# Warm-up products, an earlier half of the exponentials, and moved transposes in an attention and expert kernel on Trainium2

## The chip, the cores and the metric

The kernel runs on one core of a Trainium2 chip. The metric is device time in microseconds (us), the median of several executions; three of the kernel before took 761.15, 761.35 and 762.45 us. A profile is one further look at one execution. The engines have short names in it: PE is TensorE's matmul, PEld its weight load, DVE VectorE, ACT ScalarE, POOL GpSimd, SP the engine that issues most transfers.

## The reference

Sixteen batches of 128 tokens with 256 features pass two stages, all in fp32.

Stage one is attention of a resampler. `x` is normalised (plain layer norm) and becomes the latents; these and a context of the same size are layer-normed again with weights and biases, and the latents are modulated by a condition vector. Queries come from the latents, keys and values from context and latents together (256 rows a batch), in 16 heads of width 64:

```python
logits = jnp.einsum('bhqd,bhkd->bhqk', q * attn_scale, k * attn_scale)
w = jax.nn.softmax(logits.astype(jnp.float32), axis=-1)
out = jnp.einsum('bhqk,bhkd->bhqd', w, v)
```

The heads are projected back to 256 features and added to `x`.

Stage two is a mixture of experts on the layer norm of that: a router picks one of 8 experts for each token, its sigmoid score scales the token, and the expert computes `(silu(t @ w1) * (t @ w3)) @ w2` with 704 hidden columns. A shared expert of the same shape runs over every token. Both are added to the tokens.

## The kernel before, in words

Every engine's order is the order in which the Python code calls its operations: nothing is scheduled afterwards. Waits between engines follow from the tiles.

**Front.** Two batches make a group; there are eight. The first group's tokens and the weights of keys (`wk`), values, queries and output are loaded by SP and ACT. `first_inputs(i)` (from line 368) takes the i-th batch of the first group: statistics and a Newton square root on DVE, normalised rows `fz` (L126), four transposes on PE (L396), and scale and shift on DVE (L402) and ACT (L404) into `kvT`. In between stand the four key units of batch 0. `inputs(1)` prepares the rows of the second group; their transposes are in `second_inputs`, which calls `transpose` (L345 to L357: eight transposes on PE, six scalings on DVE) and starts the next loads.

**Units.** `k_unit` (L432) makes two of eight pairs of heads' keys: four fp32 products of 256 columns, shown as eight PE records, into one PSUM tile, which ACT copies to `kT` (L440). `v_unit` (L451, copy L458) and `q_unit` (L417, copy L424) do it for values and queries. All these tiles come from one PSUM pool, `ps_m`, with three buffers: the fourth tile waits until the first was emptied. A matmul of the first tokens' transposes, of the output projection and of the shared expert takes its tile from this pool too.

**Steps.** `step(u, units, ...)` handles half of the heads of one batch, so 32 steps. PE computes scores `S` in two tiles (L484). DVE takes maxima (`nmx`, L496), ACT the exponentials (`pe`, L503) with their sums, DVE the reciprocals (`rs`, L513), POOL the scaling (L516). Two halves (`n` = 0 and 1) pass this one after the other. `turn` transposes the probabilities in 32x32 blocks on DVE (L525) and stores them; `fetch` loads them back as `pT`; one step later `weigh` multiplies them by the values (`O`, L549). Between these, `step` calls one unit at a time so that PE has work: one after the first half's exponentials, one after the second half's, one after the second `normalise`, further ones before `turn`, the last after it.

**Last group.** In steps 28 to 31 there are no keys and queries of a next group left, and units of the shared expert fill in: `hidden` (products `p`, `pr` at L148, Silu into `sl` on ACT at L163 and L168, product `mid` on DVE at L164 and L169). Exp and Silu are in different tables of ACT, and a change is an `ACT_TABLE_LOAD`. A one-element exponential (`spare`, L792) opens each of these steps and brings Exp's table back early. `finish` is the output projection (`pw`, L565, added at L569); `norms` puts the layer norm of earlier tokens on DVE as side work.

**After it** come the rest of the shared expert (`ys`, L178, is its down projection), the routing on DVE, and 20 tiles of 128 sorted tokens through the experts (`u`, L1156, and `yr`, L1208), whose weights are loaded when attention's buffers are free.

Of the kernel before, what the change touches and what calls it, by code (L numbers as in the profile page):

```python
# [9 lines left out]
F32 = mybir.dt.float32  # L10
# [7 lines left out]
P = 128  # L18
EPS = 1e-5
RSQRT_SEED = float(0x5F3759DF)  # L20
G = 128


@with_exitstack
def resampler_attn__then__top1_moe_kernel(
# [17 lines left out]
    nc = tc.nc  # L43
# [8 lines left out]
    FC = F // P  # L52
# [4 lines left out]

    NSUB = NT // G + E - 1
    NTILE = -(-NSUB * G // P)
    GP = P // G  # L60
    TB = 2 * P
# [3 lines left out]
    NF = FC + 1  # L65
    assert G == P and NF % 2 == 0 and FR == 2 * BL and F <= 512 * 2

# [3 lines left out]
    mwork = ctx.enter_context(tc.tile_pool(name="mwork", bufs=2, side="right"))  # L71
    ps_s = ctx.enter_context(tc.tile_pool(name="ps_s", bufs=2, space=PSUM))
    ps_m = ctx.enter_context(tc.tile_pool(name="ps_m", bufs=3, space=PSUM))
# [10 lines left out]
            }  # L84
        )
    )

    ident = const.tile([P, P], F32, name="ident")
    make_identity(nc, ident)
# [17 lines left out]
    def newton(pool, v, n, tag):  # L107
# [5 lines left out]
        yi = pool.tile([P, n], I32, tag=tag + "i", name=tag + "i")  # L113
        nc.vector.tensor_scalar(yi, seed, -1.0, RSQRT_SEED, ALU.mult, ALU.add)
        y = yi.bitcast(F32)
# [129 lines left out]
    with ExitStack() as at:  # L245
# [226 lines left out]
        def logits(u):  # L472

            b, half = u // 2, u % 2
            pes[u] = work.tile([P, HS, 2 * S], F32, tag="pe", name=f"pe_{u}")
            sums[u] = small.tile([P, HS], F32, tag="sums", name=f"sums_{u}")
            ps = []
            for n in range(2):
                pl = ps_s.tile([P, 2, 2, 2 * S], F32, tag="S", name=f"S_{u}_{n}")
                for j in range(2):  # L480
                    k = 4 * half + 2 * n + j
                    for r in range(2):
                        rows = slice(r * HD, (r + 1) * HD)
                        nc.tensor.matmul(  # L484
                            pl[:, r, j, :],
                            lhsT=qTs[b // 2][rows, k, b % 2, :],
                            rhs=kTs[b][rows, k, :],
                            start=True,
                            stop=True,
                        )  # L490
                ps.append(pl)
            return ps

        def maxima(u, n, pl):
            nmx = small.tile([P, 2, 2], F32, tag="nmx", name=f"nmx_{u}_{n}")
            nc.vector.tensor_reduce(nmx, pl, AX.X, ALU.max, negate=True)  # L496
            return nmx

        def exponents(u, n, pl, nmx):
            for j in range(2):  # L500
                for r in range(2):
                    h = 4 * n + 2 * j + r
                    nc.scalar.activation(  # L503
                        pes[u][:, h, :],
                        pl[:, r, j, :],
                        AF.Exp,
                        bias=nmx[:, r, j : j + 1],
                        accum_out=sums[u][:, h : h + 1],
                    )

        def normalise(u, n):
            rs = small.tile([P, 4], F32, tag="rs", name=f"rs_{u}_{n}")
            nc.vector.reciprocal(rs, sums[u][:, ts(n, 4)])  # L513
            for i in range(4):
                w = pes[u][:, 4 * n + i, :]
                nc.gpsimd.tensor_scalar(w, w, rs[:, i : i + 1], None, ALU.mult)  # L516

        def turn(u, n):

            px = work.tile([P, NB, 2, HS // 2, BL], F32, tag="px", name=f"px_{u}_{n}")
            for t in range(2):
                nc.vector.transpose(  # L525
                    px[:, :, t].rearrange("p j h q -> p h j q"),
                    pes[u][:, ts(n, 4), ts(t, S)].rearrange("p h (j k) -> p h j k", k=BL),
                )
            nc.sync.dma_start(
                out=p_blocks[u % 2][n].rearrange("i k j x -> (i k) (j x)"),  # L530
                in_=px.rearrange("p j t h q -> p (j t h q)"),
            )

        def fetch(u):
            pTs[u] = work.tile([P, 2, NB, 2, HS // 2, BL], F32, tag="pT", name=f"pT_{u}")
            for n in range(2):
                nc.sync.dma_start(
                    out=pTs[u][:, n].rearrange("p i t h q -> p i (t h q)"),
                    in_=p_blocks[u % 2][n].rearrange("i k j x -> (k j) i x"),
                )  # L540
# [17 lines left out]
        def keep_heads(u):  # L558
            outT[u] = work.tile([P, NP // 2, S], F32, tag="oT", name=f"oT_{u}", bufs=3)
            nc.vector.tensor_copy(outT[u], heads_out.pop(u))  # L560

        def finish(b):
            pw = ps_m.tile([P, D], F32, tag="mm", name=f"pw_{b}")
            for k in range(NP):
                nc.tensor.matmul(  # L565
                    pw, lhsT=outT[2 * b + k // 4][:, k % 4, :], rhs=wo[:, k, :], start=(k == 0), stop=(k == NP - 1)
                )
            xr = xres[b // 2][:, b % 2, :]
            nc.vector.tensor_tensor(xr, pw, xr, ALU.add)  # L569
# [201 lines left out]
            a, b, c, fetch, d = [x + y for x, y in zip(t, h)]  # L771
            return a, b + ([iterate] if nt + nh else []), c, fetch, d

        def step(u, units, side, loads=(), early=4, behind=()):

            units, side = list(units), list(side)

            def aside(n):  # L780
                for f in side[:n]:
                    f()
                del side[:n]

            def unit():
                if units:
                    units.pop(0)()

            ps = logits(u)
            if u // 2 >= B - 2:  # L790

                nc.scalar.activation(spare[0:1, 1:2], spare[0:1, 0:1], AF.Exp)  # L792
            if u > 1:
                keep_heads(u - 2)
            nm = maxima(u, 0, ps[0])
            exponents(u, 0, ps[0], nm)
            nm = maxima(u, 1, ps[1])
            unit()
            for f in loads:
                f()  # L800
            normalise(u, 0)
            exponents(u, 1, ps[1], nm)
            unit()
            normalise(u, 1)
            aside(early)
            unit()
            aside(len(side))
            while len(units) > 1:
                unit()
            turn(u, 0)  # L810
            turn(u, 1)
            fetch(u)
            for f in behind:
                f()
            unit()
            if u > 0:
                weigh(u - 1)
# [21 lines left out]
        for g in range(NG):  # L839
            b0, b1 = 2 * g, 2 * g + 1  # L840
            q = [lambda j=j: q_unit(g + 1, j) for j in range(4)]
            k1 = [lambda j=j: k_unit(b1, j) for j in range(4)]
            v1 = [lambda j=j: v_unit(b1, j) for j in range(4)]
            k2 = [lambda j=j: k_unit(b1 + 1, j) for j in range(4)]
            v2 = [lambda j=j: v_unit(b1 + 1, j) for j in range(4)]
            wo_before = [lambda: finish(b0 - 1)] if g else []
            wo_first = [lambda: finish(b0)]
            na, nb, nn, back, nd = norms(g + 2 if g + 2 < NG else None, g - 1 if g else None)
            if g == 0:
                step(0, k1 + [second_inputs] + q[:2], [])  # L850
                load_shared()
                v1 = [lambda j=j: v_unit(0, j) for j in range(1, 4)] + v1
                na, nb = [], na + nb
            elif g + 1 < NG:
                step(2 * b0, k1 + q[:2] + choose, na)
            if g + 1 < NG:
                step(2 * b0 + 1, v1[:2] + wo_before + v1[2:], nb, early=0 if g else 4)
                step(2 * b1, k2 + q[2:], nn)
                ahead = [lambda: load_tokens(g + 3)] if g + 3 < NG else []
                step(2 * b1 + 1, v2[:2] + wo_first + v2[2:], [], back + ahead, behind=nd)  # L860
            else:

                sh = [shared_unit]
                step(2 * b0, k1 + sh * 2 + choose, [])
                step(2 * b0 + 1, sh * 2 + wo_before + sh * 3, nb, early=0)
                step(2 * b1, v1 + sh * 2, nn)
                step(2 * b1 + 1, sh * 2 + wo_first + sh, [], back, behind=nd)
            choose = [moe_inputs(g - 1)[2]] if g else []
        keep_heads(2 * B - 2)
        for j in range(NP // 2):  # L870
# [59 lines left out]
    def route():  # L930
# [66 lines left out]
        tiles_i = mscratch.tile([P, E], I32, name="tiles_i")  # L997
        nc.vector.tensor_scalar(tiles_i, total, float(G - 1), None, ALU.add)
        nc.vector.tensor_scalar(tiles_i, tiles_i, G.bit_length() - 1, None, ALU.arith_shift_right)
        tiles = mscratch.tile([P, E], F32, name="tiles")  # L1000
# [344 lines left out]
```

## Time and profile before

| what | us |
|---|---|
| median of three executions | 761.35 |
| the profiled execution | 762.45 |
| its span, first to last instruction | 760.6 |
| PE busy | 743.1 |
| POOL, DVE, ACT busy | 315.1, 414.1, 264.3 |
| first transposes on PE start | 7.87 |
| first key products start | 9.39 |
| step 29's scores start | 452.38 |

A timeline row gives the start, the time that the row covers, the engine, the line in the code, the operation, what it writes and reads, shapes and the number of instructions merged; in brackets stands how long the engine was idle before it and what ended the wait. A row of the waits gives who waited for whom: the sum in us, the number of times and the longest. A PE record lasts longer than the distance to the next one, since matmuls overlap; what a stream costs is read from the distance of starts.

### The profile page before, as it was taken

Reading aid. Unit: us, or ns where it says so; the run is one execution under the profiler, and the core shown is the slowest. Engines: PE = TensorE matmul, PEld = TensorE weight load, DVE = VectorE, ACT = ScalarE, POOL = GpSimd, SP = SyncE. Lnnn points to the kernel's source line nnn. Section 1 sums busy time; section 2 is a strip of 40 time slices with the busy share of each in tenths; the row PEclk is TensorE's granted clock in tenths of the full one; section 3 lists DMA queues with packets and bytes.
Section 4 is the critical chain, followed back from the end, with each engine's and each line's share of the span. In section 5 each row is a group of like instructions: output and inputs, shape, how many; then the busy total and the mean of one; then the engine's idle time right before and its main releaser. Section 6 shows DMA issues by size and latency. Waiting matters only on the chain.

```text
span 760.6 us, 11735 instructions
## 1 busy us (share of the span) xinstructions
PE 743.1 (98%) x4044; PEld 569.8 (75%) x4044; DVE 414.1 (54%) x1011; ACT 264.3 (35%) x783; POOL 315.1 (41%) x366
## 2 busy tenths in 40 slices
PE   5999999999999999999999999999999999999997
PEld 4758678677677677677677686788888777777776
DVE  4466558548647647656646456434732555555431
ACT  2544544444354353354354355711311111011111
POOL 1273464464355355445545544531012334443331
PEclk9999999999999999999999999999999999999999
DMA  8075734844943943863853644632997576776751
GB/s 291 1 238 194 221 124 160 264 146 153 262 168 134 279 170 125 240 218 125 226 200 131 185 151 140 201 139 88 383 381 261 131 200 182 212 190 184 184 155 55
DMA packets 182066, 142.48 MB, mean 187 GB/s; under 512 B 95152, under 2 KB 165811, under 8 KB 182004
## 3 DMA queue, kind: packets, MB, share of 16 engines
q1 hardware_dynamic: 175460, 125.07, 52.7%
q0 software_dynamic: 4528, 13.18, 5.5%
q10 hardware_dynamic: 2016, 3.43, 1.3%
q8 instruction: 35, 0.57, 0.3%
q14 instruction: 27, 0.22, 0.1%
HBM read 84.50 MB, written 57.67 MB: 187 GB/s over the span
## 4 chain that ended last, share of the span: by engine, by line
PE 73%; DMA 14%; DVE 4%; issue 4%; ACT 3%; POOL 1%; POOLq 0%; DVEq 0%; ACTq 0%; SPq 0%
PE pk L432 15%; PE pv L451 14%; PE S L484 7%; PE pq L417 7%; DMA out_dram<-sg,table 7%; PE O L549 7%; PE pw L565 6%; PE p L148 6%; DMA sg<-s_rows,table 5%; PE ys L178 4%; PE u L1156 3%; ACT pe L503 1%; DVE px L525 1%; PE yr L1208 1%; ACT L163 1%
## 5 line engine op out<-in xcount | busy, mean ns | idle before, releaser
L516 POOL TENSOR_SCALAR pe<-pe,rs 128x256 f32<-128x256 f32 x256 | 232.9, 931 | 255.3 <-DVE rs L513 255.3
L503 ACT ACTIVATE pe<-S,nmx 128x256 f32<-128x256 f32 x256 | 118.9, 489 | 133.0 <-DVE nmx L496 133.0
L432 PE MATMUL pk<-kvT,wk 128*128 128x256 f32 x512 | 117.4, 388 | 0.4 <-DVE kvT L402 0.4
L451 PE MATMUL pv<-wv,kvT 128*128 128x512 f32 x256 | 116.5, 599 | 0.8 <-ACT v L458 0.6
L432 PEld LDWEIGHTS pk<-kvT,wk 128*128 128x128 f32 x512 | 97.8, 194 | 18.9 <-DVE px L525 2.0
L1156 PE MATMUL u<-w13s,xT 128*128 x320 | 97.8, 459 | 0.0
L525 DVE STREAM_TRANSPOSE px<-pe 128x512 f32<-128x512 f32 x128 | 81.2, 682 | 29.6 <-POOL pe L516 29.6
L451 PEld LDWEIGHTS pv<-wv,kvT 128*128 128x128 f32 x256 | 47.2, 190 | 54.4 <-issue 51.1
L1156 PEld LDWEIGHTS u<-w13s,xT 128*128 128x128 f32 x320 | 60.8, 190 | 30.7
L496 DVE TENSOR_REDUCE nmx<-S 128x4 f32<-128x1024 f32 x64 | 75.1, 1214 | 9.4 <-PE S L484 9.4
L148 PE MATMUL p<-hT,ws 128*128 128x256 f32 x320 | 73.6, 382 | 0.8 <-DVE mid L164 0.5
L148 PEld LDWEIGHTS p<-hT,ws 128*128 128x128 f32 x320 | 59.9, 190 | 10.4 <-ACT v L458 1.2
L549 PEld LDWEIGHTS O<-pT,v 128*64 128x64 f32 x1024 | 55.2, 137 | 15.5 <-issue 12.9
L1166 ACT ACTIVATE rsl<-u 128x352 f32<-128x352 f32 x40 | 18.6, 464 | 130.6 <-PE u L1156 121.5
L484 PE MATMUL S<-kT,qT 64*128 64x256 f32 x512 | 63.9, 389 | 0.0
L549 PE MATMUL O<-pT,v 128*64 128x128 f32 x1024 | 63.2, 276 | 0.5 <-DMA pT<-p_blocks 0.5
L513 DVE RECIPROCAL rs<-sums 128x4 f32<-128x4 f32 x64 | 11.3, 177 | 91.8 <-ACT pe L503 91.8
L458 ACT COPY v<-pv 128x512 f32<-128x512 f32 x64 | 38.1, 601 | 62.9 <-PE pv L451 62.9
L417 PE MATMUL pq<-kvT,wq 128*128 128x256 f32 x256 | 58.0, 380 | 1.3 <-DVE kvT L357 1.3
L565 PE MATMUL pw<-wo,oT 128*128 128x256 f32 x256 | 57.9, 379 | 0.0
L565 PEld LDWEIGHTS pw<-wo,oT 128*128 128x128 f32 x256 | 48.6, 190 | 12.2 <-issue 3.1
L503 ACT ACTIVATION_READ_ACCUMULATOR pe<-S,nmx 128x1 f32 x256 | 56.3, 220 | 0.0
(201 smaller groups left out, 779.5 us busy)
## 6 DMA issues: line engine op xcount, KB each, us to landing
p_blocks<-px SPq DMA_DIRECT2D x64, 512.0 KB, 3.2
pT<-p_blocks SPq DMA_DIRECT2D x64, 512.0 KB, 4.2
w13s<-in_w_dram SPq DMA_DIRECT2D x16, 704.0 KB, 11.1
m_blocks<-body SPq DMA_DIRECT2D x20, 384.0 KB, 2.5
mT<-m_blocks SPq DMA_DIRECT2D x20, 384.0 KB, 3.8
wds<-in_w_dram SPq DMA_DIRECT2D x8, 640.0 KB, 12.4
t_blocks<-tx SPq DMA_DIRECT2D x12, 256.0 KB, 2.8
kvT<-t_blocks SPq DMA_DIRECT2D x12, 256.0 KB, 5.8
```

The source lines that it names most:

```text
L148: nc.tensor.matmul(ps, lhsT=shared["w13"][:, c, ds(col, P)], rhs=hT[:, c, ts(t, TB)], start=(c == 0), stop=(c == DC - 1),)
L417: nc.tensor.matmul(pq[:, jj], lhsT=wq[:, c, ts(2 * j + jj, P)], rhs=kvTs[g][:, c, :, 1, :], start=(c == 0), stop=(c == DC - 1),)
L432: nc.tensor.matmul(pk[:, jj, :], lhsT=wk[:, c, ts(2 * j + jj, P)], rhs=kvTs[b // 2][:, c, b % 2].rearrange("p t s -> p (t s)"), start=(c = ...
L451: nc.tensor.matmul(pv, lhsT=kvTs[b // 2][:, c, b % 2, t, :], rhs=wv[:, c, ts(n, 512)], start=(c == 0), stop=(c == DC - 1),)
L484: nc.tensor.matmul(pl[:, r, j, :], lhsT=qTs[b // 2][rows, k, b % 2, :], rhs=kTs[b][rows, k, :], start=True, stop=True,)
L496: nc.vector.tensor_reduce(nmx, pl, AX.X, ALU.max, negate=True)
L503: nc.scalar.activation(pes[u][:, h, :], pl[:, r, j, :], AF.Exp, bias=nmx[:, r, j : j + 1], accum_out=sums[u][:, h : h + 1],)
L516: nc.gpsimd.tensor_scalar(w, w, rs[:, i : i + 1], None, ALU.mult)
L525: nc.vector.transpose(px[:, :, t].rearrange("p j h q -> p h j q"), pes[u][:, ts(n, 4), ts(t, S)].rearrange("p h (j k) -> p h j k", k=BL),)
L549: nc.tensor.matmul(o[r * HD : (r + 1) * HD, j, :], lhsT=vs[b][:, t, ts(2 * (4 * half + j) + r, HD)], rhs=pTs[u][:, j // 2, :, t, 2 * (j % ...
L565: nc.tensor.matmul(pw, lhsT=outT[2 * b + k // 4][:, k % 4, :], rhs=wo[:, k, :], start=(k == 0), stop=(k == NP - 1))
L1156: nc.tensor.matmul(pl[:, m, 0:FH], lhsT=xT[:, c, :], rhs=w13s[:, ds(e, 1), c, ds(m * F + n * FH, FH)].rearrange("p e f -> p (e f)"), start ...
```

## The change

Three edits. First, ahead of everything else a tile is set to zero on DVE and PE multiplies it nine times by itself into a PSUM tile that nobody reads; the tile takes one of the two buffers that later hold `mid`. Second, `step` has a new argument `exp_first`: with it the first half's `normalise` and the second half's exponentials are called before the first unit instead of after it. Steps 29 and 31 use it, and in step 30 one of two shared units goes between the second and third value unit. Third, in step 0 `second_inputs` is called after the second of four key units rather than after the fourth.

```diff
+WARM = 9
...
+    idle = mwork.tile([P, FC + 1, TB], F32, tag="mid", name="idle")
+    nc.vector.memset(idle[:, 0, :], 0.0)
+    idle_ps = ps_m.tile([P, TB], F32, tag="mm", name="idle_ps")
+    for _ in range(WARM):
+        nc.tensor.matmul(idle_ps, lhsT=idle[:, 0, 0:P], rhs=idle[:, 0, :], start=True, stop=True)
...
-        def step(u, units, side, loads=(), early=4, behind=()):
+        def step(u, units, side, loads=(), early=4, behind=(), exp_first=False):
...
             nm = maxima(u, 1, ps[1])
+            if exp_first:
+                normalise(u, 0)
+                exponents(u, 1, ps[1], nm)
             unit()
             for f in loads:
                 f()
-            normalise(u, 0)
-            exponents(u, 1, ps[1], nm)
+            if not exp_first:
+                normalise(u, 0)
+                exponents(u, 1, ps[1], nm)
             unit()
...
-                step(0, k1 + [second_inputs] + q[:2], [])
+                step(0, k1[:2] + [second_inputs] + k1[2:] + q[:2], [])
...
-                step(2 * b0 + 1, sh * 2 + wo_before + sh * 3, nb, early=0)
-                step(2 * b1, v1 + sh * 2, nn)
-                step(2 * b1 + 1, sh * 2 + wo_first + sh, [], back, behind=nd)
+                step(2 * b0 + 1, sh * 2 + wo_before + sh * 3, nb, early=0, exp_first=True)
+                step(2 * b1, v1[:2] + sh + v1[2:] + sh, nn)
+                step(2 * b1 + 1, sh * 2 + wo_first + sh, [], back, behind=nd, exp_first=True)
```

## The prediction

> **What bounds the kernel now.** First the page's busy times, then the waits of PE, then the timeline at the three places that the diff touches.
>
> ```profile
> PE 743.1 (98%) x4044; PEld 569.8 (75%) x4044; DVE 414.1 (54%) x1011; ACT 264.3 (35%) x783; POOL 315.1 (41%) x366
> ```
>
> ```profile
> PE fkvt L396 <- DVE fz L126: 7.9, 1, 7.9
> PE pq L417 <- DVE kvT L357: 1.3, 2, 0.9
> PE pr L148 <- DVE mid L164: 0.8, 1, 0.8
> PE pv L451 <- ACT v L458: 0.6, 1, 0.6
> PE O L549 <- DMA pT<-p_blocks: 0.5, 1, 0.5
> ...
> PE ys L178 <- DVE mid L164: 0.4, 1, 0.4
> ```
>
> PE is occupied for 98% of the span, and its waits after the first add up to some 5 us. So PE sets the end, and time is won only where PE stands still or runs slowly. Two of the three edits aim at these waits, the third at slow running, which the waits do not show. First tokens:
>
> ```profile
> 7.87 1.13 PE L396 MATMUL fkvt<-ident,fz 128*128 128x128 f32 x4 [7.87 <-DVE fz L126]
> 9.39 9.78 PE L432 MATMUL pk<-kvT,wk 128*128 128x256 f32 x32 [0.40 <-DVE kvT L402]
> ...
> 30.59 7.17 PE L432 MATMUL pk<-kvT,wk 128*128 128x256 f32 x32
> ```
>
> The same 32 records take 9.78 us at the start and 7.17 us later: 2.6 us lost. Cut into stretches, the first of these runs shows 6 records in 10 to 12 and in 12 to 14 us, and 10 and 11 in the next two stretches; single starts lie 0.427 us apart until 14.7, then 0.216. Next the transposes of group two, between step 0's key and query units:
>
> ```profile
> 35.19 0.64 ACT L440 COPY kT<-pk 128x512 f32<-128x512 f32 x1
> ...
> 38.37 0.27 PE L346 MATMUL kvt<-ident,z 128*128 128x128 f32 x1
> ...
> 39.57 0.67 PE L417 MATMUL pq<-kvT,wq 128*128 128x256 f32 x2 [0.93 <-DVE kvT L357]
> 40.56 3.29 PE L417 MATMUL pq<-kvT,wq 128*128 128x256 f32 x14 [0.33 <-DVE kvT L357]
> ```
>
> The queries wait for VectorE to scale the tile just transposed. Last, step 29:
>
> ```profile
> 456.87 1.28 ACT L163 ACT_TABLE_LOAD   x1
> 458.16 0.38 ACT L163 ACTIVATE sl<-p 128x256 f32<-128x256 f32 x1
> 458.56 1.28 ACT L503 ACT_TABLE_LOAD   x1
> 458.58 0.42 DVE L164 TENSOR_TENSOR mid<-p,sl 128x256 f32<-128x256 f32 x1 [2.63 <-ACT sl L163]
> 458.92 0.17 DVE L513 RECIPROCAL rs<-sums 128x4 f32<-128x4 f32 x1
> ...
> 464.00 1.13 PE L148 MATMUL pr<-hT,ws 128*128 128x256 f32 x4 [0.80 <-DVE mid L164]
> 464.20 3.63 POOL L516 TENSOR_SCALAR pe<-pe,rs 128x256 f32<-128x256 f32 x4 [1.30 <-DVE rs L513]
> ```
>
> ScalarE goes to Silu's table and back between the two halves of the exponentials, and the first reciprocal (458.92) stands, in VectorE's order, behind a product that waits for that Silu, though its sums were there at 456.9.
>
> **What the Trainium skill says.** "TensorE: Matmul & The Clock Gate", section Part 1: TensorE runs at half rate until a window of about 3.4 us was busy; the windows run freely. The trace agrees on half rate (0.427 against 0.216). Part 4 there: transposes do not count as busy. That fits: the rate doubled 5.3 us after the first product of keys, 6.8 after the first transpose. "ScalarE: Activation LUTs", What ACT_TABLE_LOAD costs: 1.283 us plus 1.38 of drain. The trace shows 1.28, and no drain beside it (458.16 follows 456.87 by 1.29).
>
> **Part 1, nine products.** A memset on VectorE, which has nothing before 3.61; then nine fp32 products of 256 columns. 16 such products in four key units are 32 records, so nine are 18. The memset of 128x256 on VectorE has no row; POOL's 64x256 takes 0.34, VectorE's scaling of 128x256 0.41; so PE starts near 1.3. At 0.427 all 18 take 7.7 and end at 9.0, 1.1 past 7.87. But if one full window suffices, it closes between 1.3+3.4=4.7 and 1.3+6.8=8.1. By then 8 to 16 records are done, the rest take 0.216: the end lies between 6.9 and 8.5. Then the four transposes lie 0.109 apart, as the second batch's at 19.01 do, against 0.24. The second half of the normalised tokens is there at 8.04, so the first pair ends 0.19 earlier than before and keys start at 9.2 (in the late case at 9.65). 32 x 0.216 = 6.9, so they end at 16.1 to 16.6, against 19.0: **2.4 to 2.8 us, I take 2.6**. Below: if zeros do not count, the products only delay, by 1.1. Above: nothing more, as keys wait for VectorE's 7.63 + 0.41 and its scaling. What comes next is there: the loads of value and query weights landed at 11.2 and 14.2, wk at 8.3. Tokens of group two landed at 18.3; VectorE, which would be at them at 18.2, loses 0.1 at most, off the path.
>
> **Part 2, group two's transposes after the second key unit.** No instruction is added; VectorE's, ScalarE's and SP's orders stay. Lost now: 38.37+0.11 to 39.57, and 40.0 to 40.56, together 1.6. That goes, since the third and fourth key units (3.45) cover the six scalings (2 us). But the pool of PSUM tiles has three buffers: the two transposes' tiles take two, and the third key unit must wait for ScalarE's copy of the second, which stands behind the second half's exponentials and ends at 35.19 + 0.64 = 35.83. PE is there at 30.59 + 16 x 0.216 + 8 x 0.11 + 0.1 = 35.0. So 0.85 comes back as a new wait, with all of PE's order behind it (the two key units, both queries, step 1's scores); ScalarE and VectorE, who wait for these, have nothing due sooner: **0.75 won**. Low end 0.4, should the copy's hand-over cost more; high end 1.6. The tokens' load for the third group on SP stands where it did, ahead of the first blocks' stores.
>
> **Part 3, exponentials first (steps 29 and 31) and one shared unit between value units (step 30).** Two table loads fewer in each step, 4 x 1.28 on ScalarE, which is not the bound; only PE's waits count. I follow step 29, the start held at 452.38. Exponentials end at 456.83 and 458.7 instead of 461.8; load until 460.0; both Silus by 460.8; the two products on VectorE end at 460.9 and 461.3. First reciprocal 456.9 (was 458.92). The second now stands behind the two products, 461.3 (was 463.86); so POOL's second half starts at 461.7 instead of 464.20. PE has its fifth unit at 461.31 and the sixth at 463.04 without the wait: **0.96 won** (starts of 462.83 and 464.00, less 0.22). VectorE's norm work, 4.5 us in series from 463.95, starts at 461.6 since the output projection is done; so the maxima of step 30 come at 470.5 instead of 472.85, 1.4 earlier against PE. There the value copies now come in time, and PE's 0.75 (476.62) and 0.49 (478.93) go. The shared unit put between costs: its tile is freed only after table load and Silu, 478.7, and PE wants it at 478.3: 0.4 back. Sum **0.8**. Step 31: the exponentials start 2.8 earlier; the Silus are over by 490.8, so the down projection does not wait (0.68 at 496.75). The last probabilities: POOL ends at 495.4 instead of 500.6, VectorE's transposes at 496.75; from 501.9 to landing before 508.93 are 7.0, so they land at 503.8, and PE wants them at 504.9: the 0.79 at 508.93 goes. Together 0.96 + 0.8 + 0.68 + 0.79 = **3.2, I take 3.0**. Ends: 1.0, if only the first wait goes; 3.6 without the 0.4. After it PE stands for 0.5 us in all from 600 on, and the expert loads are issued after the same work, so they shift along.
>
> **Sum.** 2.6 + 0.75 + 3.0 = 6.3. The profiled execution took 762.45, its span 760.6; it would take 756.1. The median shown is 761.35, 1.1 lower: **755.0**.
>
> **Rivals.** *A, the clock.* Zeros do not open the gate, or it falls shut between the last product (6.9) and the keys (9.2): at most 2.4 us with nothing but transposes, less than a window. Then the front gains nothing or costs up to 1.1: 757.6 to 758.7. *B, buffers.* Step 29's Silu starts 1.9 later, so PSUM tiles come free later; by my count at 460.9 against a want at 461.3, only 0.4 to spare. If VectorE's order eats that, part 3 gives 1.2: 756.8. *C, slower.* The gate stays shut long after the gap. Part 1 of the skill's TensorE page reports a gate stuck for over 50 us; no run here shows it. At half rate PE loses half of the time. Against the 3.75 of parts 2 and 3, the slow stretch must last 7.5 us longer than now, beyond 22.2 instead of 14.7; from there the kernel is slower. With 30 us more it would lose 15 less 3.75: 772.6.
>
> **How the numbers follow.** Likeliest 0.68 (own range 753.6 to 756.6), A 0.13, B 0.14, no effect of any part 0.02, C 0.03. The range 753.4 to 758.4 takes in A mostly and B. Faster by over 0.2% (1.5 us, what a measurement can tell): 0.68 + 0.13 + 0.12 = 0.93; same 0.04; slower 0.03.
>
> **What would show it.** Right: the first 32 key records in about 7.0 us, from 9.2; a new wait of PE in the third key unit for ScalarE of 0.8 and none at the first queries; in steps 29 and 31 one table load after eight exponentials; no wait of PE for mid or for the last probabilities. Wrong: 0.427 spacing after 9.2 (A), PE waiting in steps 29 to 31 for mid or v (B), a long stretch at half rate (C).

## The result and the profile after

| | before | after |
|---|---|---|
| median of six executions, us | 761.49 | 755.98 |
| lowest to highest | 760.87 to 763.08 | 755.33 to 756.15 |
| span of the profiled execution | 760.6 | 753.6 |

The ratio is 0.9923, with a 95% interval of 0.991 to 0.9936: the kernel is 0.77% faster, 5.5 us by the medians and 4.9 to 6.9 by the interval. The forecast was 755.0, range 753.4 to 758.4. The spans of the two profiled executions differ by 7.0, which is 1.5 more than the medians: the profiled execution of before (762.45) lies 0.96 above the median of its six, that of after (755.33) 0.65 below. The experiments show where a part of this comes from.

Where did the time of the two profiles go? The starts of the stages on PE say it, in us from the span's start.

| from, to | before | after | won |
|---|---|---|---|
| start to step 0's scores | 28.66 | 25.80 | 2.87 |
| step 0's scores to step 1's | 15.12 | 14.32 | 0.80 |
| step 1's scores to step 29's | 408.59 | 408.59 | 0.00 |
| step 29's scores to step 30's | 16.31 | 15.25 | 1.06 |
| step 30's scores to step 31's | 15.79 | 14.89 | 0.90 |
| step 31's scores to the first expert tile | 105.31 | 104.07 | 1.24 |
| first expert tile to the end | 170.85 | 170.70 | 0.15 |

The page's busy times of the kernel after, then its waits of PE (who waited for whom: sum in us, times, longest):

```profile
PE 744.9 (99%) x4062; PEld 572.3 (76%) x4062; DVE 414.9 (55%) x1012; ACT 258.9 (34%) x779; POOL 315.2 (42%) x366
```

```profile
PE fkvt L404 <- DVE fz L134: 0.8, 1, 0.8
PE pk L440 <- ACT kT L448: 0.7, 1, 0.7
PE p L156 <- DVE mid L172: 0.7, 2, 0.5
```

The 18 records more are the nine products. Of the waits seen before, those of the queries (`pq`), of `pr`, `pv`, `O` and `ys` are gone. The wait of `pk` for ScalarE's `kT` is new, and so is one for `mid` in step 30 (0.17 of the 0.7; the other 0.5 comes much later and stands in both kernels). These rows count only the time in which PE had nothing at all. By the distances of starts the new waits cost 0.85 and 0.34. The timeline at the first tokens:

```profile
1.26 5.70 PE L94 MATMUL idle_ps<-idle 128*128 128x256 f32 x18 [1.26 <-DVE idle L91]
7.72 0.78 PE L404 MATMUL fkvt<-ident,fz 128*128 128x128 f32 x4 [0.77 <-DVE fz L134]
9.15 7.14 PE L440 MATMUL pk<-kvT,wk 128*128 128x256 f32 x32 [0.65 <-DVE kvT L410]
```

The products are over before the first tokens are normalised, with 0.77 us to spare; the transposes after them take 0.78 instead of 1.13 us, and the 32 key records 7.14 instead of 9.78. The first starts of the products lie 0.427 apart; from 4.4 us on, 0.216. Next the transposes of the second group, in step 0:

```profile
32.04 0.27 PE L354 MATMUL kvt<-ident,z 128*128 128x128 f32 x1
32.33 0.63 ACT L448 COPY kT<-pk 128x512 f32<-128x512 f32 x1
...
33.01 3.72 PE L440 MATMUL pk<-kvT,wk 128*128 128x256 f32 x16 [0.69 <-ACT kT L448]
...
36.57 3.62 PE L425 MATMUL pq<-kvT,wq 128*128 128x256 f32 x16
```

The queries follow the keys without a wait. The third key unit stands still until ScalarE's copy of the second ends at 32.96. And step 29:

```profile
453.21 0.18 DVE L521 RECIPROCAL rs<-sums 128x4 f32<-128x4 f32 x1 [0.93 <-ACT pe L511]
...
455.02 1.28 ACT L171 ACT_TABLE_LOAD   x1
456.31 0.66 ACT L171 ACTIVATE sl<-p 128x256 f32<-128x256 f32 x2
...
457.74 3.63 POOL L524 TENSOR_SCALAR pe<-pe,rs 128x256 f32<-128x256 f32 x4 [0.61 <-DVE rs L521]
...
459.37 1.03 PE L156 MATMUL pr<-hT,ws 128*128 128x256 f32 x4
```

One table load where there were three in this piece (456.87, 458.56 and 461.81). Counted from the step's scores (448.70, before 452.38), the first reciprocal comes at 4.5 instead of 6.5, POOL's second half at 9.0 instead of 11.8, and `pr` at 10.7, without a wait, instead of 11.6.

### The profile page after: what moved, and what is told of

Same layout as the page of the kernel before. It is cut to its first block, busy times and chain, and to the rows that moved or that the text cites. A ratio compares the mean times of both kernels' runs of the same rounds, so it can differ in the third digit from the quotient of the medians.

```text
span 753.6 us, 11767 instructions
## 1 busy us (share of the span) xinstructions
PE 744.9 (99%) x4062; PEld 572.3 (76%) x4062; DVE 414.9 (55%) x1012; ACT 258.9 (34%) x779; POOL 315.2 (42%) x366
## 4 chain that ended last, share of the span: by engine, by line
PE 78%; DMA 12%; issue 4%; DVE 3%; ACT 2%; POOL 1%; POOLq 0%; SPq 0%; DVEq 0%; ACTq 0%
PE pk L440 15%; PE pv L459 14%; PE S L492 8%; PE O L557 8%; PE p L156 8%; PE pw L573 7%; PE pq L425 7%; DMA out_dram<-sg,table 6%; DMA sg<-s_rows,table 5%; PE ys L186 5%; PE u L1169 3%; PE yr L1221 1%; ACT pe L511 1%; PE pr L628 1%; PE pr L156 1%
## 5 line engine op out<-in xcount | busy, mean ns | idle before, releaser
L440 PE MATMUL pk<-kvT,wk 128*128 128x256 f32 x512 | 115.0, 382 | 1.3 <-ACT kT L448 0.7
L440 PEld LDWEIGHTS pk<-kvT,wk 128*128 128x128 f32 x512 | 95.9, 190 | 19.1 <-DVE px L533 2.0
```

Of the source, the lines that this page charges most:

```text
L440: nc.tensor.matmul(pk[:, jj, :], lhsT=wk[:, c, ts(2 * j + jj, P)], rhs=kvTs[b // 2][:, c, b % 2].rearrange("p t s -> p (t s)"), start=(c = ...
```

## The experiments

Two theories were to be told apart. **P**: each part wins what the two profiles show for it: 2.9, 0.8 and 3.2. **W**: the moment at which TensorE's full rate begins differs between executions, the profiled execution of before had a late one, and in the median the first part wins less. W rests on the free windows of 3.4 us that the prediction draws on. Besides, each term of the sum was to be tested on its own. Each experiment was measured beside the kernel before, whose medians were 762.01 (the first three and two products), 761.66 (third key unit, steps 29 and 30) and 761.97 (the last two); ratios are therefore safer to compare than times.

### The nine products alone

```diff
+WARM = 9
...
+    for _ in range(WARM):
+        nc.tensor.matmul(idle_ps, lhsT=idle[:, 0, 0:P], rhs=idle[:, 0, :], start=True, stop=True)
```

> The nine products alone. Theory P (what the two profiles say): the key products of the first batch run at full rate from 9.15, 2.9 us are won against the profile of before, and the median falls by as much, to about 758.6. Theory W (the moment at which the clock opens differs from one execution to the next, and the profiled execution of before had a late one): the slow stretch of before is shorter in most executions, so the median falls by 1.6 to 2.2 us only, and the executions lie closer together than those of before.

Measured: 760.29 against 762.01, ratio 0.9975 (0.9966 to 0.9985): 1.7 us won in the medians, 1.1 to 2.6 by the interval. The nine executions lie between 759.62 and 760.90, those of before between 760.77 and 764.18. So 2.9 is not the typical gain. That the executions lie closer together, as W says, is only a hint, as there are nine against thirty-eight. The keys run at full rate here too:

```profile
1.26 7.04 PE L93 MATMUL idle_ps<-idle 128*128 128x256 f32 x18 [1.26 <-DVE idle L90]
9.39 7.14 PE L439 MATMUL pk<-kvT,wk 128*128 128x256 f32 x32 [0.65 <-PE fkvt L403]
```

In this execution the full rate came at 7.1 instead of 4.4. The products took 7.04, the transposes waited for them, and the keys start 0.24 later than in the profile of the changed kernel, but still at full rate.

### The transposes alone

```diff
-                step(0, k1 + [second_inputs] + q[:2], [])
+                step(0, k1[:2] + [second_inputs] + k1[2:] + q[:2], [])
```

> The moved transposes alone. Theory P: 0.75 us won (1.6 of waits for VectorE gone, a new wait of 0.85 for ScalarE's copy in the third key unit), in the profile and in the median. Rival: the edit wins more, 1.4, as the copy is not what PE waits for; or nothing, as the wait only moves. Without products the first keys run slowly until a moment that the profile shows: theory W expects it to differ from 14.7 by up to 3 us.

Measured: 761.29 against 762.01, ratio 0.999 (0.9982 to 0.9998): 0.7 won, as theory P has it. The interval, 0.2 to 1.4 us, hardly excludes the rivals (1.4 or nothing); the trace does. Step 0 takes 14.31 from scores to scores instead of 15.12, 0.81 less, and PE loses 0.85 between the last transpose and the third key unit. Its first keys, in the timeline:

```profile
9.49 9.25 PE L432 MATMUL pk<-kvT,wk 128*128 128x256 f32 x32 [0.40 <-DVE kvT L402]
```

### The last group alone

```diff
+            if exp_first:
+                normalise(u, 0)
+                exponents(u, 1, ps[1], nm)
...
+                step(2 * b0 + 1, sh * 2 + wo_before + sh * 3, nb, early=0, exp_first=True)
+                step(2 * b1, v1[:2] + sh + v1[2:] + sh, nn)
+                step(2 * b1 + 1, sh * 2 + wo_first + sh, [], back, behind=nd, exp_first=True)
```

> The exponentials ahead in steps 29 and 31 with the shared unit of step 30 moved, and nothing else. Theory P: 3.2 us won, all between the scores of step 29 and the end of step 31's last product with the values, in the profile and in the median. Rival B (buffers): about 1.2. Theory W expects the slow stretch of the first keys to end at another moment than 14.7, and the median to fall by the full 3.2 since this part does not depend on it.

Measured: 758.41 against 762.01, ratio 0.9952 (0.9939 to 0.9965): 3.6 in the medians. From step 29's scores to the first expert tile its trace needs 134.17 us, that of before 137.41: 3.24. Rival B with its 1.2 is out. The other four traces whose last group is that of before need 137.39 to 137.89, and the mean of the five is 137.65: against that, 3.5 are won, close to the 3.6 of the medians. What differs among the five is shown below, with the second profile of before. Its first keys:

```profile
9.46 9.04 PE L435 MATMUL pk<-kvT,wk 128*128 128x256 f32 x32 [0.40 <-DVE kvT L405]
```

The three parts alone give 0.25, 0.10 and 0.48%, together 0.83%; the whole change 0.77% (0.64 to 0.90). They add up within the intervals.

### Two products instead of nine

> Two products of zeros in place of nine, nothing else changed. They last 4 x 0.43 = 1.7 us, half a window. If a busy window opens the clock, they do nothing: slow records until 12 to 15 us, time as before (within 0.3 us). If what counts is only that PE worked once early (first weight load, first fetch of its instructions), two are as good as nine: about 2 us won.

The edit is to the kernel before: two products, and neither of the other parts.

Measured: 762.43 against 762.01, ratio 1.0002 (0.9994 to 1.0009): nothing won. So it isn't the early first work of PE that helps, but enough of it:

```profile
1.26 2.08 PE L93 MATMUL idle_ps<-idle 128*128 128x256 f32 x4 [1.26 <-DVE idle L90]
9.24 8.99 PE L439 MATMUL pk<-kvT,wk 128*128 128x256 f32 x32 [0.44 <-DVE kvT L409]
```

### The kernel before, profiled a second time

> One more look at the kernel before. Theory W: the slow records of the first keys end at another moment than 14.7, somewhere between 12.8 and 16.2 (a window of 3.4 us after 9.4, whose start is free), and the span differs by half of the difference.

Measured: one execution of 762.28, span 760.6. Its first keys:

```profile
9.29 9.40 PE L432 MATMUL pk<-kvT,wk 128*128 128x256 f32 x32 [0.40 <-DVE kvT L402]
```

With this there are five traces in which the keys begin at the low rate. The change of rate is read from the starts of single records; where it falls between two starts, it is placed by the distance of the two:

| trace | first key product | full rate from | 32 records, us | over 7.14 |
|---|---|---|---|---|
| before, as first profiled | 9.39 | 14.69 | 9.78 | 2.64 |
| before, second profile | 9.29 | 13.84 | 9.40 | 2.26 |
| transposes alone | 9.49 | 13.73 | 9.25 | 2.11 |
| last group alone | 9.46 | 13.27 | 9.04 | 1.90 |
| two products | 9.24 | 12.99 | 8.99 | 1.85 |

The loss is half of the slow stretch in each, and it ranges over 0.8 us from trace to trace. The profile that the prediction was made from has the largest; the mean of the five is 2.15. With the products, the full rate came at 4.4, 5.0, 5.7, 6.2, 7.1, 7.1 and 7.4 in seven traces, and the keys start between 9.15 and 9.51 (where nine products stand). Theory W holds in its core: the moment is not fixed, all five lie between the 12.8 and 16.2 that were expected, and the profiled pair is a late one against an early one. From the start to step 0's scores, four traces without products took 27.99 to 28.66 (mean 28.27) and six with nine 25.80 to 26.15 (mean 25.95): 2.3 won on average, where the profiled pair shows 2.87.

That the change of rate is one of TensorE's clock is on record, too. The trace's record of the granted clock begins with an entry of full clock, and this entry starts at the moments of the table to within 0.02 us; nothing is recorded ahead of it. After the last product an entry of half the clock follows. In the twelve traces the entry of full clock lasts 744.11, 747.52 or 750.93 us, which is 218, 219 or 220 times 3.413. So the clock changes on a grid of steps of 3.41 us, and where this grid lies against the kernel's start differs between executions.

The expectation that the span follows with half of the difference failed: step 0's scores come 0.47 earlier in the second profile, and the span is nearly the same. The traces show why. A second loss varies, the one in front of the second half of the last probabilities in step 31:

```profile
508.93 1.09 PE L549 MATMUL O<-pT,v 128*64 128x128 f32 x16 [0.53 <-DMA pT<-p_blocks]
508.79 1.09 PE L549 MATMUL O<-pT,v 128*64 128x128 f32 x16 [0.86 <-DMA pT<-p_blocks]
```

The first line is of the first profile, the other of the second. From the last product of the first half to the first of the second half it is 0.10 us where nothing waits. In the five traces with the last group of before it is 0.79, 0.80, 1.14, 1.23 and 1.33, and apart from this place their last groups agree within 0.1 us. The profile that the prediction was made from has the largest loss of the first kind and nearly the smallest of the second. Why the load lands later in some executions was not tried.

### The transposes after the third key unit

```diff
-                step(0, k1[:2] + [second_inputs] + k1[2:] + q[:2], [])
+                step(0, k1[:3] + [second_inputs] + k1[3:] + q[:2], [])
```

> The changed kernel with the second group's transposes after the third key unit instead of the second. If PE's new wait there is for a PSUM buffer (three in the pool, the third key unit needs the one that ScalarE empties at the end of the second half's exponentials), then one unit later that buffer and the next are free when PE comes to them: the wait of 0.85 goes, the first query waits 0.2 to 0.3 for VectorE instead, and 0.5 us are won against the changed kernel: about 755.5. If PE waits there for something else, the 0.85 stays and the time is that of the changed kernel; if the queries' wait for VectorE comes back in full, it is 0.8 slower.

Measured: 755.05, ratio 0.9911 (0.9896 to 0.9925) against 0.9923 for the changed kernel; in the trace step 0 takes 13.43 from scores to scores, instead of 14.32: 0.89 won there. The intervals of the two kernels overlap, so that the trace and not the median carries this. The timeline:

```profile
32.38 0.63 ACT L448 COPY kT<-pk 128x512 f32<-128x512 f32 x1
...
33.93 1.96 PE L440 MATMUL pk<-kvT,wk 128*128 128x256 f32 x8
35.73 3.62 PE L425 MATMUL pq<-kvT,wq 128*128 128x256 f32 x16
```

No wait stands at the fourth key unit nor at the queries. The new wait of the change was for a PSUM buffer, then: with one unit more ahead, the same copy (32.38 to 33.01) is over when PE needs its buffer, now for the second tile of transposes at 33.49. The fourth key unit takes the third's buffer, whose copy ends at 33.85, just before PE comes at 33.93. The 0.2 to 0.3 expected at the first query did not come.

### Step 30's units as before

```diff
-                step(2 * b1, v1[:2] + sh + v1[2:] + sh, nn)
+                step(2 * b1, v1 + sh * 2, nn)
```

> The changed kernel with step 30's units as before (four value units, then two shared ones). By the prediction the moved unit costs 0.4 (its PSUM tile is freed only after a table load and a Silu) and wins nothing, since the earlier maxima alone free the value tiles: 0.3 to 0.4 us faster than the changed kernel, and PE's wait before the second shared unit of step 30 is gone. Rival: the unit between the value units is what makes ScalarE's copies come in time; without it the waits of 0.75 and 0.49 come back and the time is 0.8 or more longer.

Measured: median 755.68 of executions from 755.14 to 759.59, ratio 0.9934 (0.9915 to 0.9953): no difference from the changed kernel that the times can tell. The trace can: step 30 takes 14.43 instead of 14.89, as expected, without PE's wait before the second shared unit. The waits of 0.75 and 0.49 for ScalarE's value copies did not come back, so the rival is out. But step 31 gives most of it back:

```profile
478.73 2.00 PE L492 MATMUL S<-kT,qT 64*128 64x256 f32 x16
...
480.62 2.34 DVE L504 TENSOR_REDUCE nmx<-S 128x4 f32<-128x1024 f32 x2
```

The maxima of step 31 (`nmx`) start 1.89 us after its scores, in the changed kernel 1.18 (480.02 after 478.84). VectorE turns both halves of the probabilities just before, where the moved unit lets it turn one half earlier. PE pays 0.32 of the 0.45 in step 31, in front of the shared unit's `pr`, so that 0.13 is left.

### The exponentials ahead in step 29 alone

```diff
-                step(2 * b1 + 1, sh * 2 + wo_first + sh, [], back, behind=nd, exp_first=True)
+                step(2 * b1 + 1, sh * 2 + wo_first + sh, [], back, behind=nd)
```

> The changed kernel with the exponentials ahead in step 29 alone; step 31 as before. The prediction puts 0.68 (down projection waiting for mid) and 0.79 (last probabilities) to step 31: 1.3 to 1.5 us slower than the changed kernel, with both waits back. Rival: step 29 alone frees step 31 too, since its exponentials start 2.8 us earlier anyway: under 0.5 us slower.

Measured: 757.06, ratio 0.9933 (0.992 to 0.9946); in the trace 135.33 us from step 29's scores to the first expert tile instead of 134.20, so 1.1 slower by the trace; the medians (757.06 and 755.98) say the same, but the intervals of the two kernels overlap. One of the two expected waits is back:

```profile
503.24 1.09 PE L557 MATMUL O<-pT,v 128*64 128x128 f32 x16 [0.93 <-DMA pT<-p_blocks]
```

Between the two halves of the last probabilities the distance of starts is 1.21 us. That lies among the 0.79 to 1.33 of the traces with the kernel before's last group, so it is the same wait come back, and not a longer one. In the six other traces in which step 31 has its exponentials ahead, the distance is 0.10. The down projection (`ys`) does not wait: step 29 had freed that already. So the edit in step 31 wins 1.1 in this pair of traces, all of it in this one wait. Neither expectation was met, since one wait came back and not both.

### Both small edits together

```diff
-                step(0, k1[:2] + [second_inputs] + k1[2:] + q[:2], [])
+                step(0, k1[:3] + [second_inputs] + k1[3:] + q[:2], [])
...
-                step(2 * b1, v1[:2] + sh + v1[2:] + sh, nn)
+                step(2 * b1, v1 + sh * 2, nn)
```

> The changed kernel with the transposes after the third key unit and step 30's units as before the change. The traces of the two single edits show 0.89 and 0.13 us won against the changed kernel. If they add: 1.0 won, about 755.0; if step 30's order does nothing in the median, the time of the first edit alone, 755.1.

Measured: 755.59, ratio 0.991 (0.9897 to 0.9924). That is the time of the first edit alone (ratio 0.9911) within what the times can tell. Its trace has step 0 at 13.43 as well, and step 30 at 14.44. But step 31, up to the first expert tile, takes 104.73 instead of 104.07: 0.31 is lost in front of `pr`, as with step 30's order alone, and 0.35 more in front of the second half of step 30's probabilities, whose load PE waits for. So in this trace step 30's old order wins nothing.

### Sixteen products

> The changed kernel with sixteen products of zeros in place of nine. 32 records from 1.26: the clock opens between 4.4 and 8.1, 7 to 16 records are slow (0.427), the others take 0.216, so the last one starts between 9.5 and 11.3 and the first transposes wait for it instead of for VectorE at 7.7. Theory P: 1.8 to 3.6 us slower than the changed kernel, about 758.5, though no key product runs slowly. Rival: the sequence of first tokens has slack that hides some of it, and the time is under 1 us longer.

Measured: 759.82, ratio 0.9964 (0.9952 to 0.9975): 3.8 slower than the changed kernel by the medians, 3.1 by the ratios. The timeline at the first tokens:

```profile
1.26 9.00 PE L94 MATMUL idle_ps<-idle 128*128 128x256 f32 x32 [1.26 <-DVE idle L91]
10.10 0.60 PE L404 MATMUL fkvt<-ident,fz 128*128 128x128 f32 x4
11.35 7.14 PE L440 MATMUL pk<-kvT,wk 128*128 128x256 f32 x32 [0.65 <-PE fkvt L404]
```

The transposes start 2.4 us and the keys 2.2 later than in the changed kernel's trace, at full rate. So the front has no slack: what overruns 7.7 is paid, 2.2 us here, inside theory P's range. The rest of the distance to the changed kernel's trace (1.5) is in the expert tiles: from the first of them to the end this trace takes 172.2, that of the changed kernel 170.7. There an expert's down projection (`yr`) loses 0.8 us waiting for the addition before it, which itself waits for gathered rows; 0.2 is lost at an earlier one, and 0.3 behind the last product.

## Why the prediction was right, and where its sizes were off

The time lies in the range and the cause is the one forecast: PE set the end, and each of the three edits takes away something that PE lost. The forecast fall of 6.3 was 0.8 too large by the medians, but it lies inside the interval (4.9 to 6.9). The size of the terms is judged from the single experiments. The first was too large and the third too small, and in the sum of 6.3 these errors partly cancel; that is luck.

- **Nine products.** The course was as worked out: a start at 1.26 (forecast 1.3), the full rate between 4.4 and 7.4 (4.7 to 8.1), keys from 9.15 to 9.51 (9.2 to 9.65), at full rate. Zeros count, so rival A did not happen, nor C. The term of 2.6 was mis-sized: it is the distance to one execution of before, whose slow stretch is the longest of five. From the start to step 0's scores the traces show 2.3 on average, and 1.7 was measured alone (1.1 to 2.6). The recorded sum also has a slip: keys that end at 16.1 instead of 19.0 win 2.9, not 2.8. The low end of 2.4 covered the moment at which the rate changes after the change, and not the same freedom before it.
- **Transposes.** 0.75 forecast, 0.80 in the trace, 0.7 in the median. The new wait was forecast at 0.85, and PE lost 0.855 there.
- **Last group.** 0.96, 0.8 and 1.47 were worked out for steps 29, 30 and 31, and 1.06, 0.90 and 1.24 came. The sum was 3.2 in both; the 3.0 taken was a discount without need. In step 31 the down projection won 0.49 and not 0.68: the forecast took the whole distance of starts in front of it, 0.69, and products that do not wait stand 0.20 apart there. The last probabilities won 0.75 (forecast 0.79), and would win 1.0 on average of the five traces, as the profile of before has nearly the smallest wait there. Step 30's second shared unit lost 0.335 (forecast 0.4). The share of `ys` (0.68) was put down to step 31's edit; the run with step 29 alone shows that step 29 frees it.
- **Rival B**, buffers in step 29, had 0.4 us to spare by the working: in the trace the first `mid` ends at about 457.1 and PE wants that buffer at 457.64. It was near, and did not come.
- **The end.** That the part behind it only shifts holds for the profiled pair (170.85 and 170.70). Over all twelve traces it took 170.3 to 172.2, with no edit in it. In five of them waits of `yr` cost 0.4 to 1.1 of that, most with sixteen products, and from the start of the last product to the end it is 4.2 to 4.9. What makes the rows come late was not tried.

## What to carry to other kernels

A single profile gives one draw of a loss that varies: where a term rests on the moment at which a rate changes, profile several executions of the kernel before, too. The same holds for a wait for a load, which here ranged from 0.8 to 1.3. Products that fill an idle start are worth it while they end before the first real work is ready. Here two did nothing, nine won about 2, though in three of six traces they ended late enough to hold up the transposes, and sixteen cost 2.2 in the front. A unit moved into a gap brings its buffers with it: count the pool's tiles at the new place, and one unit later may be better.

## What was unexpected of the hardware

The clock rose on a grid of 3.41 us, as the lengths of the full-clock entries show. "TensorE: Matmul & The Clock Gate" (Part 1) gives the same free-running window, 3413 ns, and a busy one as what raises the clock. How full a step has to be can be estimated from the traces. In the changed kernel's trace the clock rose at 4.42, so the step before it began at 1.01. PE had products from 1.26 on, 93% of the step, and that was enough. In the run with step 30's units as before, the clock rose at 7.38. The step from 0.55 to 3.97, with products from 1.26 on, was filled to 79%, and that was not enough.

Whether transposes count as work, these traces do not tell; the prediction found its moments fitting for "no", but they fit "yes" nearly as well. In the first profile of before, the step from 7.87 to 11.28 was filled to 88% if they count and to 55% if not, and the clock did not rise.

In the changed kernel PE had only the four transposes for 2.2 us between the products and the keys (6.96 to 9.15), and the clock stayed. At the end of the twelve traces it fell 2.5 to 5.3 us after the last product, so a pause little longer than this one can be enough to lose it.
